# Ordering steps behind three engines' queues, placing the ternary weights, and the lead of the gathered rows in a 12-sublayer decoder

## The chip, the cores and the metric

The kernel runs on one core of one Trainium2 chip. The metric is the time of one execution on the device in microseconds (us), as the median of several executions. A core has a matrix engine (TensorE, PE; its weight loads are listed as PEld), a vector engine (VectorE, DVE), a scalar engine (ScalarE, ACT), a general engine (GpSimd, POOL) and a sync engine (SyncE, SP) that here issues DMAs. Each engine works through its own queue in order; engines wait for each other by semaphores.

## The reference

A decoder of four layers with three sublayers each, on 8192 tokens of width D = 128. Each sublayer is added to its input and normalised. The change touches the first three sublayers, and the planning ahead of the last one:

```python
# L0 attn: mixture of experts, the best 2 of 8 for each token
logits = x @ gate_w + gate_b;  probs = softmax(logits)
topw, topi = top_k(probs, 2);  topw = topw / topw.sum(-1)
hid = gelu(einsum('nd,edf->enf', x, w1) + b1)
out = einsum('enf,efd->end', hid, w2) + b2
x = layernorm(x + sum over the two experts of out * topw)
# L0 xattn: one head, context of 64 rows per sequence
x = layernorm(x + softmax(q @ k.T * scale) @ v)
# L0 ffn: ternary weights
t(w) = w + (clip(round(w / mean(abs(w))), -1, 1) - w)
x = layernorm(x + gelu(x @ t(W1).T + b1) @ t(W2).T + b2)
...
# L3 ffn: the best 1 of 8 experts, with a capacity for each expert
```

## The kernel before

The tokens lie in 16 chunks of 512 (four tiles of 128 tokens). The twelve sublayers run in the order of a list at the end of `tile_decoder`. The tile framework orders each engine's instructions by a scheduler; `tc.issue_after(ins)` puts what is made in its block behind `ins` on that instruction's own engine, without making it wait for anything else. Without such an edge, the scheduler may place an instruction among others as it likes, so far as data allow.

**Mixture of experts** (class `Sorted`, L472). Only the chosen experts are computed. A `plan` sorts the pairs of token and expert into groups of 256 rows that share an expert. There are two batches: chunks 0 to 4 with 27 groups and chunks 5 to 15 with 51. For each group n, `all_groups` (L860) does these steps:
- `load(n + 2)` (L727): SP reads a register with the expert's number and issues two DMAs, weights `rw` (512 KB, L738) and biases `aux` (66 KB, L739).
- `rows(n + 3)` (L742): DVE copies the row indices (`rat`, L755), POOL issues two indirect DMAs that gather 128 rows each (L757) into one of eight places in the four `aux` tiles.
- `turn(n + 1)` (L763): PE transposes the rows (`ebT_ps`, L768), DVE copies them (`ebT`, L770).
- `hidden(n)` (L772): PE multiplies (`h_ps`, L782), ACT applies GELU (L784).
- `output(n - 1)` (L787): PE multiplies (`yg`, L795), DVE adds the bias (`yo`, L796), SP stores 128 KB to `l_rout` in DRAM (L797).
- `between`: a hook; here `context` (L920) loads the context `cin` (256 KB per chunk) in the last 32 groups.
- The steps laid aside: the plan of the next batch, whose last step is due four groups before the end (`total - 4`), and the sums (`finish`, L802) of the batch before, spread by `stretch`. They are queued behind the last instruction of `Sorted` on each engine.

`finish` reads back, tile by tile, the two outputs of each token: DVE copies indices (`fat`, L815), POOL gathers two `got` tiles (L817), DVE adds them to x (`r`, L827 and L829) and takes statistics (L830). At the end of a chunk `end` (L832 to L847) finds 1/sqrt by integer steps on DVE (`fln`, `rt_u`, L348 to L357) and applies the normalisation in `ln_apply` (L372): on ACT (L378, after one more DVE operation `lns`, L375), on POOL or on DVE (L380).

What remains of the sums after the groups is `moe_end`. `moe_done(c)` (L936) runs it until chunk c is finished.

**One-head cross attention with the ternary FFN** (`xattn_single`, L984). It makes the ternary weights of the FFN first: `ternary(n)` (L1062 to L1080) for two matrices of 128 x 512, each with one ACT operation, a reduction (`terns`, L1067), a matmul (L1069) and eight DVE operations. Its loop (L1108 to L1116) interleaves the steps of several chunks: scores(i+1), summed, turned(i-2), turned_weights(i), projections(i+2), summed, hidden(i-2), summed, values(i), sources(i+3), output(i-2), summed. `summed` takes one step of `moe_end`, so the MoE's sums end in this loop, four steps (one chunk) in a turn. `sources` calls `moe_done`. The matmuls `y` at L1048 end the attention of a chunk; r at L1054 adds them to x. PE's operations that the prediction names are the score values `v_ps` (L1003, L1008), the transposes `xT_ps` (L325) and the FFN's `h_ps` (L1093) and `y` (L1103).

**Masked attention and switch.** The plan of the last sublayer's first batch (`switch_begin`) is made during the masked attention (`mha`, L1130): the hook `aside` calls `kept` (L1916), which takes a few steps at each of four places of a chunk, behind instructions that `mha` hands to it (`seen`). Its operations are named `plan`, `pln`, `pli`, `plw`.

Of the kernel before, what the change touches and what calls it, by code (L numbers as in the profile page):

```python
# [22 lines left out]
P = 128  # L23
# [208 lines left out]


@with_exitstack
def tile_decoder(ctx: ExitStack, tc: tile.TileContext, a, out):
# [9 lines left out]
    mm = nc.tensor.matmul  # L245
    V, A, G = nc.vector, nc.scalar, nc.gpsimd

# [38 lines left out]
    def load_weights(n):  # L286

        if 0 < n < 11:
            name = LAYER_WEIGHTS[n - 1]
            parts = []  # L290
            for o in range(0, _NBLOCKS[name], 8):
                k = min(8, _NBLOCKS[name] - o)
                parts.append(work("wts", (P, k, P), f"w_{name}{o}"))
                nc.sync.dma_start(out=parts[-1], in_=a["w_" + name][:, o : o + k, :])
            W[n] = parts[0] if len(parts) == 1 else parts

    def table(name, shape, src):
# [14 lines left out]
    make_identity(nc, ident)  # L312


    def bank(name):
# [156 lines left out]
    class Sorted:  # L472
# [4 lines left out]
        def __init__(s, which, top, batches, src, wg, bias, act, cap=None, store=False, scattered=None):  # L477
            s.which, s.top, s.batches, s.src, s.wg, s.bias, s.act, s.cap, s.store = which, top, batches, src, wg, bias, act, cap, store
            s.at, s.loaded, s.done, s.carry = {}, {}, set(), None
# [322 lines left out]
        def finish(s, b):  # L802
# [29 lines left out]
            def end(i):  # L832
                r, st = sums.pop(i)
                got.pop(i)
                f = sm.tile([P, 4, TPC], F32, tag="fln", name="fln")
                mv = f[:, :2].rearrange("p a t -> p (a t)").rearrange("p (t a) -> p t a", a=2)
                v, y = f[:, 2], f[:, 3]
                for t in range(TPC):
                    V.bn_aggr(mv[:, t, :], st[:, t, :])  # L839
                s.dve = V.tensor_scalar(v, mv[:, :, 1], LN_EPS, None, ALU.add)  # L840
                yield
                for ins in rsqrt_steps(v, TPC, y):
                    s.dve = ins
                    yield
                ln_apply(cs[i], r, mv, y, s.store, on_act=True)
                s.done.add(cs[i])
                yield  # L847
# [12 lines left out]
        def all_groups(s):  # L860
# [3 lines left out]
            s.ring = work("e", (P, 8, 2, D), "yo")  # L864
            for n in range(3):
                s.rows(n)
# [4 lines left out]
            for b in range(nb):  # L871
# [68 lines left out]

# [41 lines left out]


    def xattn_single():  # L984
        w = W[1]
        scale = 1.0 / math.sqrt(D)

        st = {}
        bv = bias_rows(row("l0xbv"), 0, "bv1")
        ring = work("e", (P, 4, TPC, D), "v1")  # L990
# [66 lines left out]

        b2 = bias_rows(row("l0fb2"), 1, "b2t")
        tern = W[2]
        wt = work("tab", (P, 2, FK, P), "tern")  # L1060

        def ternary(n):  # L1062
            src = tern[:, 4 * n : 4 * n + 4, :].rearrange("p k m -> p (k m)")
            t = work("tmp", (P, 512), "absw")
            s = sm.tile([P, 1], F32, tag="terns", name="terns")
            A.activation(t, src, AF.Abs)
            V.tensor_reduce(s, t, AX.X, ALU.add)  # L1067
            ps = bank("tern_ps")
            mm(ps[:, 0:1], sq[:, 2, :], s, start=True, stop=True)  # L1069

            V.tensor_scalar(s, ps[:, 0:1], 1.0 / (D * FF), 1e-8, ALU.mult, ALU.max)
            V.reciprocal(s, s)
            df = wt[:, n].rearrange("p k m -> p (k m)")
            V.tensor_scalar(df, src, s, None, ALU.mult)
            V.tensor_scalar(df, df, -1.0, 1.0, ALU.max, ALU.min)

            V.tensor_scalar(df, df, 12582912.0, None, ALU.add)
            V.tensor_scalar(df, df, 12582912.0, None, ALU.subtract)
            V.tensor_tensor(df, df, src, ALU.subtract)
            V.tensor_tensor(df, df, src, ALU.add)  # L1080

        def summed(_):
            next(moe_end, None)

# [23 lines left out]
        for i in range(-3, NC + 2):  # L1108
            for step, c in (
# [19 lines left out]

    def mha(prepare, wv, finish, mask=None, diff=False, aside=lambda c, k, seen: None):  # L1130

# [164 lines left out]
        nlam = lam_neg() if diff else None  # L1296
        on, late, spread = range(NC), (), None
        for c in range(-2, NC + 1):
            last = finish(c - 1, st[c - 1]) if c - 1 in on else iter(())
            behind = None  # L1300
            if c in on:
                behind = weights(c, 0)
            for _ in late:
# [3 lines left out]
            if c - 1 in on:  # L1307
                values(c - 1, 1)
            aside(c, 0, (behind, spread))
# [5 lines left out]
            aside(c, 1, (seen, spread))  # L1315
            if c in on:
                weights(c, 1)
                behind = values(c, 0)
            aside(c, 2, (behind, spread))
            if c + 1 in on:  # L1320
                scores(c + 1, 1)
                split_maxima(c + 1)
            if c + 2 in on:
                spread = project(c + 2)
            next(last, None)
# [5 lines left out]
            late = last if diff else ()  # L1331
            aside(c, 3, (seen, spread))
            st.pop(c - 1, None)
# [581 lines left out]

    def kept(c, k, seen):  # L1916

# [46 lines left out]
```

## Time and profile before

| | |
|---|---|
| median of 18 runs | 3300.52 us (3290.14 to 3305.32) |
| profiled execution | 3298.73 us |
| its span, from the first to the last instruction | 3297.0 us |
| mean granted PE clock | 0.948 |
| busy, PE / PEld / DVE / ACT / POOL | 2909.4 / 2119.3 / 2016.3 / 1642.1 / 1463.5 us |
| first group's `h_ps` / last group's, about | 65 / 434 us |
| cross attention and ternary FFN, about | 438 to 735 us |
| masked attention, about | 2700 to 3035 us |

The page gives for each group of instructions the line, engine, operation, tile written and tiles read. "Idle before" is the time that the engine stood still ahead of an instruction, and the arrow names what ended it. A list of waits sums these. In a table of windows each engine's busy time in a stretch stands beside the granted clock (1.00 is full speed), the share of the DMA engines that was busy and what they moved. Tile names are shown without their numbers.

### The profile page before, as it was taken

Reading aid. Unit: us, or ns where it says so; the run is one execution under the profiler, and the core shown is the slowest. Engines: PE = TensorE matmul, PEld = TensorE weight load, DVE = VectorE, ACT = ScalarE, POOL = GpSimd, SP = SyncE. Lnnn points to the kernel's source line nnn. Section 1 sums busy time; section 2 is a strip of 40 time slices with the busy share of each in tenths; the row PEclk is TensorE's granted clock in tenths of the full one; section 3 lists DMA queues with packets and bytes.
Section 4 is the critical chain, followed back from the end, with each engine's and each line's share of the span. In section 5 each row is a group of like instructions: output and inputs, shape, how many; then the busy total and the mean of one; then the engine's idle time right before and its main releaser. Section 6 shows DMA issues by size and latency. Waiting matters only on the chain. (4 is left out here: it accounts for less than half of the span.)

```text
span 3297.0 us, 110598 instructions
## 1 busy us (share of the span) xinstructions
PE 2909.4 (88%) x47136; PEld 2119.3 (64%) x47136; DVE 2016.3 (61%) x7344; ACT 1642.1 (50%) x3138; POOL 1463.5 (44%) x1500
## 2 busy tenths in 40 slices
PE   5898888998899899999999989998999569998983
PEld 3788755666666677766677767774444336766883
DVE  3732256766777666532346655666888886675245
ACT  3443355765444455433345645553445555654443
POOL 2565554334555444311134453557566323436234
PEclk9999988999999899999999999999999789998997
DMA  4577731000000200000000000000000000002674
GB/s 132 157 201 209 223 83 30 21 8 3 3 3 10 84 4 4 6 1 1 1 15 4 4 5 4 4 6 7 1 1 2 8 1 16 18 14 71 193 236 135
DMA packets 142461, 159.26 MB, mean 48 GB/s; under 512 B 16720, under 2 KB 118096, under 8 KB 141968
## 3 DMA queue, kind: packets, MB, share of 16 engines
q1 hardware_dynamic: 128064, 123.66, 12.7%
q0 software_dynamic: 13184, 27.03, 3.0%
q8 instruction: 370, 6.06, 0.8%
q10 hardware_dynamic: 720, 1.50, 0.1%
q14 instruction: 123, 1.01, 0.1%
HBM read 121.45 MB, written 30.67 MB: 46 GB/s over the span
## 5 line engine op out<-in xcount | busy, mean ns | idle before, releaser
L1213 DVE TENSOR_REDUCE m<-s_ps 128x8 f32<-128x512 f32 x640 | 397.5, 683 | 143.6 <-PE s_ps L1441 49.3
L1262 ACT ACTIVATE e<-t_ps 128x512 f32<-128x512 f32 x640 | 330.0, 602 | 150.3 <-PE t_ps L1255 149.8
L1280 PE MATMUL av_ps<-vx,e 128*64 128x18 f32 (+1 forms) x10240 | 335.8, 215 | 6.2 <-issue 6.0
L1280 PEld LDWEIGHTS av_ps<-vx,e 128*64 128x64 f32 x10240 | 317.8, 139 | 26.1 <-issue 19.0
L784 ACT ACTIVATE hT<-h_ps,aux 128x256 f32<-128x256 f32 x496 | 206.4, 469 | 247.2 <-issue 157.9
L1157 POOL TENSOR_SCALAR eb<-qT,small 128x512 f32<-128x512 f32 x80 | 130.6, 1632 | 422.4 <-ACT qT L960 200.6
L817 POOL DMA_INDIRECT got<-l_rout,fat x192 | 192.5, 1003 | 222.4 <-DVE fln L839 64.4
L1243 PE MATMUL t_ps<-eb,kT 32*64 32x128 f32 x10240 | 281.9, 285 | 4.6 <-DVE m L1213 2.3
L380 POOL TENSOR_SCALAR x<-xb,lnmv,ln_y 128x128 f32<-128x128 f32 x240 | 188.4, 797 | 175.6 <-DVE ln_y L345 169.1
L782 PE MATMUL h_ps<-ebT,rw 128*128 128x256 f32 x992 | 246.9, 394 | 19.5 <-DVE ebT L770 16.1
L795 PEld LDWEIGHTS yg<-rw,hT 128*128 128x128 f32 x1984 | 244.9, 194 | 6.9
L1243 PEld LDWEIGHTS t_ps<-eb,kT 32*64 32x64 f32 x10240 | 199.3, 132 | 71.5 <-DVE m L1213 25.5
L795 PE MATMUL yg<-rw,hT 128*128 128x128 f32 x1984 | 244.7, 277 | 0.0
L1205 PE MATMUL s_ps<-eb,qT 32*64 32x256 f32 x5120 | 216.9, 397 | 20.2 <-POOL eb L1157 9.6
L757 POOL DMA_INDIRECT aux<-in_x_dram,rat x156 | 159.0, 1019 | 125.6 <-DVE rat L755 43.2
L782 PEld LDWEIGHTS h_ps<-ebT,rw 128*128 128x128 f32 x992 | 185.3, 197 | 45.2 <-DVE ebT L770 20.1
L380 POOL TENSOR_SCALAR x<-r,lnmv,ln_y 128x128 f32<-128x128 f32 x100 | 79.6, 808 | 296.9 <-DVE ln_y L345 250.5
L796 DVE TENSOR_TENSOR yo<-yg,aux 128x256 f32<-128x256 f32 x124 | 52.4, 422 | 254.6 <-PE yg L795 254.5
L1285 DVE RECIPROCAL rc<-av_ps 128x32 f32<-128x32 f32 (+1 forms) x192 | 61.7, 321 | 236.9 <-PE av_ps L1280 236.5
L1155 ACT ACTIVATE eb<-qT,small 128x512 f32<-128x512 f32 x160 | 106.8, 715 | 128.4 <-POOL qT L1382 123.7
L1157 POOL TENSOR_SCALAR eb<-kT,small 128x512 f32<-128x512 f32 x80 | 144.8, 1810 | 21.5 <-ACT kT L962 11.0
L1205 PEld LDWEIGHTS s_ps<-eb,qT 32*64 32x64 f32 x5120 | 113.5, 134 | 60.2 <-issue 15.6
(443 smaller groups left out, 6502.1 us busy)
## 6 DMA issues: line engine op xcount, KB each, us to landing
rw<-in_l0w_dram SPq DMA_DIRECT2D x78, 512.0 KB
rw<-in_l3w_dram SPq DMA_DIRECT2D x46, 512.0 KB
l_rout<-yo SPq DMA_DIRECT2D x124, 128.0 KB
aux<-xd SPq DMA_DIRECT2D x46, 128.0 KB
aux<-in_l0b_dram SPq DMA_DIRECT2D x78, 66.0 KB
xd<-vx SPq DMA_DIRECT2D x5, 1024.0 KB
x<-in_x_dram SPq DMA_DIRECT2D x16, 256.0 KB
cin<-in_ctx_dram SPq DMA_DIRECT2D x16, 256.0 KB
```

What stands on the lines that cost most here:

```text
L380: (V if on_dve else G).tensor_scalar(X[c][:, t, :], r[:, t, :], mv[:, t, 0:1], y[:, t : t + 1], ALU.subtract, ALU.mult)
L757: s.gather = G.indirect_dma_start(out=eb[:, i, :], out_offset=None, in_=x[:, :], in_offset=bass.IndirectOffsetOnAxis(ap=at[:, i : i + 1], ...
L782: s.pe = mm(ps[:, j * GR : (j + 1) * GR], w1[:, (k + j) * P : (k + j + 1) * P], ebT, start=True, stop=True)
L784: s.act_ins = A.activation(hT[k + j], ps[:, j * GR : (j + 1) * GR], s.act, bias=v[:, k + j : k + j + 1])
L795: s.pe = mm(y[:, i * P : (i + 1) * P], hT[k][:, i * P : (i + 1) * P], w2[:, k, :], start=(k == 0), stop=(k == FK - 1))
L817: s.gather = G.indirect_dma_start(out=got[i][k][:, t, :], out_offset=None, in_=s.rout[b][:, :], in_offset=bass.IndirectOffsetOnAxis(ap=at[ ...
L1157: ins = (G if h == 2 else V).tensor_scalar(dst, x, mine, None, ALU.mult)
L1205: mm(ps[g][j * S : (j + 1) * S, u * 256 : (u + 1) * 256].rearrange("p (h k) -> p h k", h=4), rows32(s["q"], g)[:, b], rows32(s["eb"], g)[: ...
L1213: last = V.tensor_reduce(s["m"][:, g, 2 * hf : 2 * hf + 2, :].rearrange("p t h -> p (t h)"), ps[g].rearrange("p (n k) -> p n k", k=S), AX. ...
L1243: mm(ps[g][i * S : (i + 1) * S].rearrange("p (a u j q) -> p a u j q", u=2, a=2, j=2)[:, :, u, j, :], rows32(s["k"], g)[:, b], rows32(s["eb ...
L1262: last = A.activation(e[:, g, :], ps[g], AF.Exp, scale=scale)
L1280: mm(av[j * S : (j + 1) * S, 8 * (u - u0) + n, :], ev[:, n // 2, n % 2, u, j, :], vx[:, 2 * (2 * hf + u) + j, n, :], start=True, stop=True,)
```

## The change

1. `V`, `A` and `G` become wrappers (`Recorded`) that remember the last instruction issued on VectorE, ScalarE and GpSimd. A new `behind(V, A, G)` queues a block behind those.
2. Each step of `moe_end` (in `moe_done` and in `summed`) and each step of `switch_begin` (in `kept`) is put behind all three. `kept` no longer gets instructions from `mha`.
3. The MoE reads the rows of a group five groups ahead instead of three (the switch, whose rows are sorted already, stays at three); the plan of the next batch is due two groups earlier.
4. The ternary weights' source (l0f, 512 KB) is loaded when 30 groups are left. The weights and two bias rows are made in 12 steps, one at each odd number of groups left below 24, behind V, A, G and the MoE's last matmul. In `xattn_single` they are no longer made.
5. After `all_groups` the rest of the sums normalises on POOL instead of ACT (`slack`).

```diff
+class Recorded:
+    def __init__(self, engine):
+        self.engine, self.last = engine, None
+    def __getattr__(self, name):
+        method = getattr(self.engine, name)
+        def call(*args, **kwargs):
+            ins = method(*args, **kwargs)
+            self.last = getattr(ins, "ins", None) or self.last
+            return ins
+        return call
...
-    V, A, G = nc.vector, nc.scalar, nc.gpsimd
+    V, A, G = Recorded(nc.vector), Recorded(nc.scalar), Recorded(nc.gpsimd)
...
-        if 0 < n < 11:
+        if 0 < n < 11 and n not in W:
...
+    def behind(*engines):
+        stack = ExitStack()
+        for e in engines:
+            if e.last:
+                stack.enter_context(tc.issue_after(e.last))
+        return stack
...
-                ln_apply(cs[i], r, mv, y, s.store, on_act=True)
+                ln_apply(cs[i], r, mv, y, s.store, on_act=not s.slack)
...
-            for n in range(3):
+            far = 3 if s.sorted else 5
+            for n in range(far):
                 s.rows(n)
...
-                    aside.append([s.plan(b + 1), s.plan_costs(b + 1), 0, 0, total - 4])
+                    aside.append([s.plan(b + 1), s.plan_costs(b + 1), 0, 0, total - far - 1])
...
-                    if n + 3 < N:
-                        s.rows(n + 3)
+                    if n + far < N:
+                        s.rows(n + far)
...
-    moe.between = context
-
     def moe_top2():
...
         moe.all_groups()
+        assert next(making, None) is None
+        moe.slack = True
 
     def moe_done(c):
         while c not in moe.done:
-            next(moe_end)
+            with behind(V, A, G):
+                next(moe_end)
...
+    def ternary(n):
+        src = W[2][:, 4 * n : 4 * n + 4, :].rearrange("p k m -> p (k m)")
...
+        A.activation(t, src, AF.Abs)
+        yield V.tensor_reduce(s, t, AX.X, ALU.add)
+        ps = bank("tern_ps")
+        moe.pe = mm(ps[:, 0:1], sq[:, 2, :], s, start=True, stop=True)
+        yield
+        V.tensor_scalar(s, ps[:, 0:1], 1.0 / (D * FF), 1e-8, ALU.mult, ALU.max)
+        V.reciprocal(s, s)
+        df = FIRST["wt"][:, n].rearrange("p k m -> p (k m)")
+        V.tensor_scalar(df, src, s, None, ALU.mult)
+        yield V.tensor_scalar(df, df, -1.0, 1.0, ALU.max, ALU.min)
+        V.tensor_scalar(df, df, 12582912.0, None, ALU.add)
+        yield V.tensor_scalar(df, df, 12582912.0, None, ALU.subtract)
+        V.tensor_tensor(df, df, src, ALU.subtract)
+        yield V.tensor_tensor(df, df, src, ALU.add)
+
+    def made_first():
+        FIRST["wt"] = work("tab", (P, 2, FK, P), "tern")
+        for n in range(2):
+            yield from ternary(n)
+        FIRST["bv"] = bias_rows(row("l0xbv"), 0, "bv1")
+        yield
+        FIRST["b2"] = bias_rows(row("l0fb2"), 1, "b2t")
+        yield
...
+    def before_single(left):
+        context(left)
+        if left == 30:
+            with moe.after(moe.sp):
+                moe.sp = load_weights(2)
+        if left < 24 and left % 2:
+            with behind(V, A, G), moe.after(moe.pe):
+                moe.dve = next(making, None) or moe.dve
+
+    moe.between = before_single
...
         def summed(_):
-            next(moe_end, None)
+            with behind(V, A, G):
+                next(moe_end, None)
...
-            if i in (-3, -2):
-                ternary(i + 3)
...
-    def kept(c, k, seen):
+    def kept(c, k):
...
-        with ExitStack() as behind:
-            for i in seen:
-                if i:
-                    behind.enter_context(tc.issue_after(i))
-            for _ in range(steps):
+        for _ in range(steps):
+            with behind(V, A, G):
                 next(switch_begin, None)
```

More of the change, by code (lines that the diff above doesn't have):

```diff
@@ L293, in load_weights @@
                 parts.append(work("wts", (P, k, P), f"w_{name}{o}"))
-                nc.sync.dma_start(out=parts[-1], in_=a["w_" + name][:, o : o + k, :])
+                ins = nc.sync.dma_start(out=parts[-1], in_=a["w_" + name][:, o : o + k, :])
             W[n] = parts[0] if len(parts) == 1 else parts
+            return ins
     def table(name, shape, src):
@@ L478, in __init__ @@
             s.which, s.top, s.batches, s.src, s.wg, s.bias, s.act, s.cap, s.store = which, top, batches, src, wg, bias, act, cap, store
-            s.at, s.loaded, s.done, s.carry = {}, {}, set(), None
+            s.at, s.loaded, s.done, s.carry, s.slack = {}, {}, set(), None, False
             s.row_tiles, s.turned, s.between, s.stretch, s.rest = {}, {}, None, 1, None
@@ L981, in bias_rows @@
         return both[:32, 0, :], both[:32, 1, None, :].to_broadcast([32, 4, D])
+    FIRST = {}
+    def ternary(n):
+        src = W[2][:, 4 * n : 4 * n + 4, :].rearrange("p k m -> p (k m)")
+        t = work("tmp", (P, 512), "absw")
+        s = sm.tile([P, 1], F32, tag="terns", name="terns")
+        A.activation(t, src, AF.Abs)
[20 more added lines that the diff above has]
+        yield
+    making = made_first()
+    def before_single(left):
[7 more added lines that the diff above has]
+    moe.between = before_single
     def xattn_single():
@@ L988, in xattn_single @@
         st = {}
-        bv = bias_rows(row("l0xbv"), 0, "bv1")
         ring = work("e", (P, 4, TPC, D), "v1")
@@ L1055, in values @@
             layernorm(c, r, on_act=True)
[L1058 to L1080, printed above, removed]
+        wt, bv, b2 = FIRST["wt"], FIRST["bv"], FIRST["b2"]
         def summed(_):
-            next(moe_end, None)
+            with behind(V, A, G):
+                next(moe_end, None)
         def turned(c):
@@ L1128, in rows32, with mha @@
         return t[32 * g : 32 * g + 32]
-    def mha(prepare, wv, finish, mask=None, diff=False, aside=lambda c, k, seen: None):
+    def mha(prepare, wv, finish, mask=None, diff=False, aside=lambda c, k: None):
         dh = 16 if diff else 8
@@ L1296, in mha @@
         nlam = lam_neg() if diff else None
-        on, late, spread = range(NC), (), None
+        on, late = range(NC), ()
         for c in range(-2, NC + 1):
             last = finish(c - 1, st[c - 1]) if c - 1 in on else iter(())
-            behind = None
             if c in on:
-                behind = weights(c, 0)
+                weights(c, 0)
             for _ in late:
@@ L1308, in mha @@
                 values(c - 1, 1)
-            aside(c, 0, (behind, spread))
+            aside(c, 0)
             seen = scores(c + 1, 0) if c + 1 in on else None
@@ L1314, in mha @@
                 project_v(c + 1)
-            aside(c, 1, (seen, spread))
+            aside(c, 1)
             if c in on:
                 weights(c, 1)
-                behind = values(c, 0)
-            aside(c, 2, (behind, spread))
+                values(c, 0)
+            aside(c, 2)
             if c + 1 in on:
@@ L1323, in mha @@
             if c + 2 in on:
-                spread = project(c + 2)
+                project(c + 2)
             next(last, None)
@@ L1331, in mha @@
             late = last if diff else ()
-            aside(c, 3, (seen, spread))
+            aside(c, 3)
             st.pop(c - 1, None)
```

## The prediction

> **What bounds the kernel now.** I read the clock and span first (3297.0 us, mean clock 0.948; the execution itself took 3298.73 us, 1.8 under the median of 3300.52), then the slices, then tables by stage. The edits touch three stages: the MoE groups (64 to 438 us), the one-head cross attention and ternary FFN (438 to 735) and the end of the masked attention (2920 to 2960). On TensorE (PE) the instructions are the same in both kernels, and so is their order behind the first 2,390 of 38,758.
>
> *Groups.* PE's timeline of an undisturbed stretch gives the floor of one group:
>
> ```profile
> 224.70 1.90 PE L782 MATMUL h_ps<-ebT,rw 128*128 128x256 f32 x8
> ...
> 228.44 1.89 PE L782 MATMUL h_ps<-ebT,rw 128*128 128x256 f32 x8
> ...
> 232.17 1.89 PE L782 MATMUL h_ps<-ebT,rw 128*128 128x256 f32 x8
> ...
> 237.72 1.90 PE L782 MATMUL h_ps<-ebT,rw 128*128 128x256 f32 x8
> ```
>
> 228.44 - 224.70 = 3.74 and 232.17 - 228.44 = 3.73 us, and then a group of 5.55. From h of group 22 (188.76) to h of group 77 (433.8) the mean is 245.0 / 55 = 4.45: 55 x (4.45 - 3.73) = 40 us above the floor. The waits of 200 to 440 us (total, times, longest) say who takes them:
>
> ```profile
> POOL got L817 <- DVE r L827: 38.6, 11, 13.5
> PEld ebT_ps L768 <- DMA aux<-in_x_dram,rat: 30.2, 22, 3.2
> ...
> PE ebT_ps L768 <- DMA aux<-in_x_dram,rat: 25.3, 18, 3.0
> ```
>
> PE waits 25.3 us for gathered rows. The rows come late because POOL's queue holds a `got` gather that waits for a free buffer (up to 13.5 us), and the row gathers stand behind it. One of these on PE's timeline:
>
> ```profile
> 297.63 1.95 PE L795 MATMUL yg<-rw,hT 128*128 128x128 f32 x16
> 302.60 0.48 PE L768 MATMUL ebT_ps<-ident,aux 128*128 128x128 f32 x1 [3.02 <-DMA aux<-in_x_dram,rat]
> ```
>
> and the windows (busy PE, PEld, DVE, ACT, POOL, then clock, DMA share, GB/s) around it, with a well-fed one ahead of them from another answer:
>
> ```profile
> 220.00:240.00 20.00, 18.33 (x125) 16.88 (x124) 4.40 (x16) 7.82 (x19) 13.96 (x14) 1.00 0.82 242
> ```
>
> ```profile
> 300.00:305.00 5.00, 2.14 (x6) 1.58 (x7) 0.56 (x3) 0.00 (x0) 3.92 (x4) 0.71 0.90 277
> 305.00:310.00 5.00, 5.00 (x25) 4.55 (x24) 0.07 (x1) 1.68 (x4) 0.00 (x0) 0.60 0.18 57
> ```
>
> The gap of 3.02 us is followed by a clock of 0.60 to 0.71. The 20-us windows' clocks of .83, .91, .91 and .83 in 200 to 440 cost about 20 x (.17+.09+.09+.17) = 10 us. 25.3 + 10 = 35 of the 40.
>
> *Cross attention.* Here chunk follows chunk by the start of the first `y` matmul (L1048): 27.0 us from chunk 2 to 3, a mean of (624.2 - 508.86)/6 = 19.2 for the next six, and 14.5 to 14.9 once the MoE sums are done, with PE 100% busy. Among the sums PE, ACT and POOL wait for late DVE work: on PE's timeline, then POOL's, then in the waits of 440 to 640:
>
> ```profile
> 443.57 0.58 PE L1003 MATMUL v_ps<-vx 32*128 32x512 bf16 x1 [4.48 <-DVE terns L1071]
> ```
>
> ```profile
> 497.64 1.01 POOL L817 DMA_INDIRECT got<-l_rout,fat  x1 [0.30 <-issue]
> 505.87 1.00 POOL L817 DMA_INDIRECT got<-l_rout,fat  x1 [7.22 <-DVE fln L839]
> ```
>
> ```profile
> POOL got L817 <- DVE fln L839: 63.5, 8, 10.2
> ACT x L378 <- DVE lns L375: 46.3, 10, 8.3
> ```
>
> **The parts.**
>
> 1. *Rows five groups ahead.* The same gathers are issued two groups (7.5 us at the floor) earlier. Their buffers allow it: the eight halves of `aux` give group n+5 the place of group n-3, whose transposes are four groups back. The lead in front of the transpose grows from two groups to four, 15 us, over the longest hold of 13.5. So PE's 35 us would go, and the floor would give -40. What is late next is the DMA. A group moves 512 + 66 (weights, biases) + 128 (rows) + 128 (store) KB, about 50 of `got`, and in the last 32 groups 128 of context: 1.01 MB, which in 3.73 us is 271 GB/s. The trace held 242 in the window above and up to 265 in the other MoE stage; at 255 these groups take 3.97 us, 32 x 0.24 = +7.6. The l0f and l1a weights now move among the groups too: 0.9 MB at 250 GB/s, +3.6. Sum -40 + 11 = **-28**. Bounds: -40 (no drag) and -8 (the 25.3 us turn into waits for weights and only most of the clock loss goes).
>
>    The Trainium skill (TensorE: Matmul & The Clock Gate, "HAM oscillation — how this bites in real kernels") puts the harmful gap at over about 3.4 us. By it gaps of 3.0 cost no clock, and this term would be -18; the 0.60 after 3.02 us says otherwise, and the trace decides.
>
> 2. *Plan of batch 1 due in 21 groups instead of 23.* DVE is 15.9 to 19.4 of 20 us busy at 120 to 180, so the plan's work sets the pace there (5.0 us a group), and packing it tighter leaves two faster groups behind it: 21 x 5.12 + 2 x 3.73 = 23 x 5.0. **0**, with +5 if it now delays transposes' copies.
>
> 3. *Ternary weights among the groups.* 16 DVE operations, per matrix .13+.15+.46+.42+.42+.42+.68+.69 = 3.4 us, two 6.7 us, leave 443 to 456, where DVE is 15.0 of 20 us busy and PE lost 4.48. They go where DVE is 4 to 6 of 20 busy, hidden by PE's 17.7 of 20. If that cover fails, each of the 12 steps holds `ebT` copies by at most one operation pair, 1.4 us: +8. **-5** (the 4.48 and a little clock); bounds -9, +3.
>
> 4. *Steps queued behind V, A and G; normalising the rest on POOL.* `moe_done` and `summed` may no longer be hoisted or spread by the scheduler, so DVE does xattn's own work in the order written, and 14 chunks' LN applies (56) leave ACT for POOL. Their prices:
>
> ```profile
> L378 ACT ACTIVATE x<-r,lns,fln x128: 477/481/536, 356.5 to 3292.8; 128x128 f32<-128x128 f32 x128
> ```
>
> ```profile
> L380 POOL TENSOR_SCALAR x<-r,lnmv,ln_y x100: 782/792/1541, 652.0 to 1681.8; 128x128 f32<-128x128 f32 x100
> ```
>
>    Four cost 1.9 us on ACT and 3.2 on POOL, and the `lns` operation on DVE goes. ACT no longer stands up to 8.3 us with its own softmax and GELU queued behind an apply; instead `got` gathers (1.00 + 0.30 each, 2.6 a pair) are queued behind the applies on POOL, and the transposes of `x` behind both. POOL's need per chunk is 4 x 2.6 + 3.2 = 13.6, under 19.2.
>    - The slump of 27.0 us should shrink to about 21, like its neighbours: **-6**; bounds -9, and +10 if the three chunks' applies (3 x 3.1) in front of the gathers of batch 1 are paid in full.
>    - The steady chunks: by the compiled order I count x ready about 8.5 us behind `y` (fln 2.6, first apply 0.8, a pair 2.6, three applies 2.4), and some 10 us of PE work behind that: 17.8 to 18.7, plus 0 to 2 for a slow clock after PE's wait. Against 19.2 over seven chunks: **-3**; bounds -8, +10.
>
>    The Trainium skill (GPSIMD Engine Reference, "Engine selection") calls one-input elementwise work on POOL roughly line-rate against VectorE. By it four applies would be near DVE's 1.1 us and the steady term about -10; the 792 ns row decides.
>
> 5. *The switch's plan in the masked attention.* The last LN chain, now in front of the plan's operations, took 5.4 us (2955.0 to 2960.4) interleaved with them and 4.0 (2930.4 to 2934.4) alone; `av_ps` starts there are 13.1 and 14.3 us apart against about 9.5 later: **-3**; bounds -8, +4.
>
> Sum: -28 + 0 - 5 - 6 - 3 - 3 = **-45**: 3298.7 - 45 = 3254 for a profiled execution, and **3255** for the median.
>
> **Rivals.**
> - *DMA and POOL become the bound of the groups.* For: 271 GB/s would be needed at the end, POOL needs 2.6 for the rows and 0.7 for sums (14 pairs of `got` over 51 groups) of 3.73 us. Against: the other MoE stage runs at 3.73 with 246 GB/s. The groups give only -12, the rest -8: 3280.
> - *All of it*: groups at the floor (-40), xattn chunks at 17 us (7 x -2.2 = -15), the slump and the ternary in full (-9, -9): 3227.
> - *Slower: POOL's queue holds `x` in the cross attention.* Each chunk's x waits for the dearer applies (3.2 - 1.9 = 1.3) and one gather pair (2.6) more: 3.9 us over the 11 chunks of batch 1 = +43. Against the groups' -28 and the ternary's -5 that is +10: 3310. It decides from 3 us a chunk, (28 + 5)/11. Against it: the applies start as soon as their statistics do, and ACT's 46.3 us of waiting went through the same chain.
> - *The lead is not real* (gathers still behind held `got` gathers, which moved ahead with them): groups 0, the rest -8 to 0: 3296, no change.
>
> **How the numbers follow.** Forecast 0.48 (3236 to 3270), all of it 0.18, DMA and POOL 0.18, no lead 0.06, slower 0.10. This kernel's measurement can tell about 0.2%, 6.6 us. The no-lead case is half faster: faster 0.48 + 0.18 + 0.18 + 0.02 = 0.86, same 0.04, slower 0.10. The range leaves out most of "slower" and the tail of "all of it": 3218 to 3292.
>
> **What would show it.** Right: h starts 3.8 to 4.0 us apart at 200 to 430, the wait of `ebT_ps` for gathered rows under 8 us, clock near 1.00 there; 434 - 30 for the last h; no PE wait on `terns`; chunk intervals of the cross attention at 17 to 19 and none over 22. Wrong: PE waiting for `rw`, DMA share over 0.9 with groups still at 4.4; PE waiting more than 3 us a chunk at `xT_ps` for POOL's `x`; chunk intervals over 20.

## The result, and the profile after

The changed kernel takes 3341.02 us (median of 7), the kernel before 3300.87 (43): ratio 1.0122, 95% interval [1.0108, 1.0136]. It is slower by 1.2%, where 1.4% faster was forecast and the range ended at 3292. The spans of the two profiled executions differ by 3338.0 - 3297.0 = 41.0 us. Four marks on PE's timelines say where it comes from (us from the span's start):

| mark | before | after | difference of the stage |
|---|---|---|---|
| last block of `yg` of the groups | 434.2 | 404.7 | -29.5 |
| last attention `y` of the cross attention | 706.3 | 725.7 | +49.0 (272.0 became 321.0) |
| first `s_ps<-mf,half` (the mask) of the masked attention | 2720.4 | 2741.7 | +1.9 |
| first `h_ps` of the switch | 3042.2 | 3082.6 | +19.1 (321.8 became 340.9) |
| end of the span | 3297.0 | 3338.0 | +0.6 |

*Groups.* All operations of DVE, ACT and POOL now carry the line L243, that of the wrapper, so they are read by tile. On PE's timeline the groups stand 3.73 us apart (215.89 - 212.16):

```profile
212.16 1.89 PE L806 MATMUL h_ps<-ebT,rw 128*128 128x256 f32 x8
...
215.89 1.89 PE L806 MATMUL h_ps<-ebT,rw 128*128 128x256 f32 x8
```

Two executions of the kernel before, in the table above and in e6 below, differ by 10 us in the first mark (434.2 and 424.0), so the groups' -29.5 is known no better than that.

No wait of PE for gathered rows is left among the waits of 200 to 440 us; the largest wait of PE for a DMA there is the one for weights:

```profile
PE h_ps L806 <- DMA rw<-in_l0w_dram: 5.3, 2, 4.1
```

and the DMA carries more than in any 20-us window of 200 to 440 us before (at most 244 GB/s). A window of 40 us; the next one has 270 GB/s:

```profile
280.00:320.00 40.00, 38.51 (x266) 35.98 (x265) 12.81 (x54) 17.41 (x42) 27.15 (x28) 1.00 0.90 278
```

*Cross attention.* Aligned by the first `y` matmul of each chunk's attention, the stage lost its time in two places, and the rest of it changed by -3 us in all:

| chunks | before | after | difference |
|---|---|---|---|
| 3 to 9 | 508.86 to 624.20, 19.2 us each | 478.91 to 616.22, 22.9 each | +22 us |
| 9 to 13 | 624.20 to 682.99, 14.7 us each | 616.22 to 704.98, 22.2 each | +30 us |

The same four stretches as windows (the clock is the third column from the end), the kernel before first:

```profile
508.90:624.20 115.30, 102.79 (x650) 69.16 (x649) 79.75 (x519) 73.87 (x148) 46.86 (x48) 0.88 0.10 28
624.20:683.00 58.80, 58.80 (x435) 39.16 (x434) 45.28 (x274) 48.68 (x97) 15.88 (x19) 1.00 0.06 19
```

```profile
478.90:616.20 137.30, 110.42 (x650) 74.46 (x649) 88.50 (x517) 66.76 (x127) 68.50 (x73) 0.80 0.09 24
616.20:705.00 88.80, 75.47 (x434) 50.33 (x433) 52.53 (x299) 45.90 (x86) 39.68 (x45) 0.81 0.07 20
```

The clock was already 0.88 before in the first stretch; after, it is 0.80. In the second stretch PE was never idle before: POOL's last `got` gather started at 631.53, and PE waited for none of the sums' last tiles. After, that gather starts at 664.62, and PE still waits for POOL's `x` at 688.15.

Among the waits of 408 to 740 us are these:

```profile
ACT xT L243 <- PE xT_ps L349: 126.5, 24, 8.8
POOL got L243 <- DVE r L243: 77.5, 15, 10.0
DVE r L243 <- PE y L1150: 72.0, 13, 8.4
...
PE xT_ps L349 <- POOL x L243: 45.7, 45, 3.7
```

PE's waits for POOL's `x` are new, and DVE waits for the FFN's `y` longer than before (72.0 us instead of 14.8 in 440 to 740); POOL's gathers waited for DVE before too (63.5 us for `fln` in 440 to 640). ACT's wait for the transposes follows from PE's. Read as a loop: PE waits for POOL's `x`; POOL's gathers, which stand ahead of `x` in its queue, wait for DVE's adds (`r`), which free their buffers; DVE waits for PE's `y` of the FFN (L1150), because that addition is queued ahead of the sums' adds. DVE's timeline, the addition of `y` at the start of a turn, a sum's add, and the next addition of `y`:

```profile
540.10 0.69 DVE L243 TENSOR_TENSOR r<-y,x 128x512 f32<-128x512 f32 x1 [4.35 <-PE y L1150]
...
546.34 0.34 DVE L243 SCALAR_TENSOR_TENSOR r<-got,plw,x 128x128 f32<-128x128 f32 x1
...
562.96 0.69 DVE L243 TENSOR_TENSOR r<-y,x 128x512 f32<-128x512 f32 x1 [7.92 <-PE y L1150]
```

PE's timeline of the same turn:

```profile
552.51 0.48 PE L349 MATMUL xT_ps<-ident,x 128*128 128x128 f32 x1 [3.43 <-POOL x L243]
...
553.45 1.65 PE L1150 MATMUL y<-tern,vx 128*128 128x128 f32 x6
555.92 0.48 PE L349 MATMUL xT_ps<-ident,x 128*128 128x128 f32 x1 [0.82 <-POOL x L243]
...
557.73 5.19 PE L1150 MATMUL y<-tern,vx 128*128 128x128 f32 x26
```

and POOL's timeline what the tiles stand behind: four gathers, the first of which waits for the sum's add, and a pair of gathers between the first apply and the other three.

```profile
546.70 0.99 POOL L243 DMA_INDIRECT got<-l_rout,fat  x1 [8.65 <-DVE r L243]
...
551.65 0.80 POOL L243 TENSOR_SCALAR x<-r,fln 128x128 f32<-128x128 f32 x1
552.63 1.08 POOL L243 DMA_INDIRECT got<-l_rout,fat  x1 [0.17 <-DVE lnst L243]
554.02 1.00 POOL L243 DMA_INDIRECT got<-l_rout,fat  x1 [0.30 <-issue]
555.07 2.35 POOL L243 TENSOR_SCALAR x<-r,fln 128x128 f32<-128x128 f32 x3
```

The windows of 5 us in this turn show the other part of the loss, the clock (third column from the end; 0.99 in the window ahead of these, 547 to 552 us):

```profile
552.00:557.00 5.00, 3.38 (x10) 2.00 (x10) 2.76 (x17) 0.00 (x0) 4.48 (x6) 0.50 0.13 39
557.00:562.00 5.00, 4.70 (x22) 4.54 (x22) 0.00 (x0) 0.59 (x1) 2.50 (x3) 0.50 0.08 26
562.00:567.00 5.00, 5.00 (x40) 3.27 (x39) 3.80 (x26) 2.86 (x7) 0.00 (x0) 0.98 0.01 3
```

PE is idle for 3.43 us, and then works for 10 us at half speed.

*End of the masked attention.* PE's first instruction of the switch, of before and then of after:

```profile
3038.45 0.66 PE L768 MATMUL ebT_ps<-ident,aux 128*128 128x128 f32 x2 [2.78 <-DMA aux<-xd]
```

```profile
3078.99 0.66 PE L792 MATMUL ebT_ps<-ident,aux 128*128 128x128 f32 x2 [15.76 <-DMA aux<-xd]
```

Its rows were scattered by POOL, 40 scatters at 0.97 + 0.30 us. Before, they ran from 2971.18 to 3033.78 and none but the first waited over 0.31 us; after, from 2996.57 to 3074.04 with holes. Counted from the stage's start (2720.4 and 2741.7) the first scatter is 4 us later, and the scatters take 15 us longer. Lines of POOL's timeline after:

```profile
3047.09 0.97 POOL L243 DMA_INDIRECT xd<-x,pli  x1 [6.02 <-DVE rc L243]
...
3062.56 0.97 POOL L243 DMA_INDIRECT xd<-x,pli  x1 [3.02 <-DVE pli L243]
```

### The profile page after: what moved, and what is told of

Read it like the earlier page. It is cut to its first block, busy times and chain, and to the rows that moved or that the text cites. A ratio compares the mean times of both kernels' runs of the same rounds, so it can differ in the third digit from the quotient of the medians.

```text
span 3338.0 us, 110655 instructions
## 1 busy us (share of the span) xinstructions
PE 2931.5 (88%) x47136; PEld 2134.3 (64%) x47136; DVE 2039.3 (61%) x7330; ACT 1621.2 (49%) x3082; POOL 1507.6 (45%) x1556
## 5 line engine op out<-in xcount | busy, mean ns | idle before, releaser
L243 DVE TENSOR_REDUCE m<-s_ps 128x8 f32<-128x512 f32 (+1 forms) x656 | 404.1, 677 | 154.1 <-PE s_ps L1485 49.3
L243 ACT ACTIVATE e<-t_ps 128x512 f32<-128x512 f32 x640 | 330.0, 601 | 150.5 <-PE t_ps L1300 150.0
L243 POOL TENSOR_SCALAR eb<-qT,small 128x512 f32<-128x512 f32 x80 | 130.4, 1630 | 423.0 <-ACT qT L243 344.8
L243 ACT ACTIVATE hT<-h_ps,aux 128x256 f32<-128x256 f32 x496 | 207.1, 470 | 225.6 <-issue 110.2
L243 POOL DMA_INDIRECT got<-l_rout,fat x192 | 194.9, 1015 | 218.9 <-DVE r L243 121.2
L243 POOL TENSOR_SCALAR x<-xb,lnmv,ln_y 128x128 f32<-128x128 f32 x240 | 188.0, 795 | 177.1 <-DVE ln_y L243 173.5
L806 PE MATMUL h_ps<-ebT,rw 128*128 128x256 f32 x992 | 246.0, 392 | 23.7 <-DVE ebT L243 13.2
L243 POOL DMA_INDIRECT aux<-in_x_dram,rat x156 | 159.8, 1024 | 114.1 <-PE h_ps L806 49.3
L243 POOL TENSOR_SCALAR x<-r,lnmv,ln_y 128x128 f32<-128x128 f32 x100 | 79.6, 809 | 286.5 <-DVE ln_y L243 259.6
L243 DVE RECIPROCAL rc<-av_ps 128x32 f32<-128x32 f32 (+1 forms) x192 | 61.7, 321 | 238.9 <-PE av_ps L1325 238.7
L243 DVE TENSOR_TENSOR yo<-yg,aux 128x256 f32<-128x256 f32 x124 | 52.4, 422 | 253.8 <-PE yg L819 253.8
L243 ACT COPY xT<-xT_ps 128x512 f32<-128x512 f32 x128 | 76.9, 601 | 240.3 <-PE xT_ps L349 239.9
L243 ACT ACTIVATE eb<-qT,small 128x512 f32<-128x512 f32 x160 | 106.8, 715 | 128.3 <-POOL qT L243 123.3
L243 POOL TENSOR_SCALAR eb<-kT,small 128x512 f32<-128x512 f32 x80 | 144.7, 1809 | 21.7 <-ACT kT L243 19.6
```

The costliest lines, as they stand in the source:

```text
L243: ins = method(*args, **kwargs)
L806: s.pe = mm(ps[:, j * GR : (j + 1) * GR], w1[:, (k + j) * P : (k + j + 1) * P], ebT, start=True, stop=True)
```

## The experiments

Two theories stood at first for the cross attention: P, that the applies on POOL are the cause, and S, that the order behind DVE's queue is. A third, C, came later: that the slow clock after each of PE's waits is a large part of it. For the planning there was K: the three edges make it late.

The runs came in five sets, each with the kernel before measured beside it; the ratios are to that. In two of the sets (e1 to e4, e13 to e16) that kernel itself took 3382 and 3385 us instead of about 3300, with more idle time of PE under "issue" (18.0 us ahead of `av_ps` in e4, 7.6 in e10, which are the same kernel) and slower groups whatever the kernel (from the 24th of the 78 groups to the last 234 to 236 us in e4, e14 and e15, 210 to 213 in the changed kernel, e5, e9 and e10). The study did not find why. So stages are compared within a set only; those two sets have no trace of the kernel before. "Stage" is from the last block of `yg` to the last attention `y` (the expectations count it from the end of that block, 3.5 us less); "planning" is from the first `s_ps<-mf,half` of the masked attention to the first `h_ps` of the switch.

| run | ratio, 95% interval | before, us | stage | planning |
|---|---|---|---|---|
| e1 kept of before | 1.0066 [1.0042, 1.0091] | 3382 | 329.4 | 364.2 |
| e2 applies on ACT | 0.9972 [0.9956, 0.9988] | 3382 | 301.5 | 372.5 |
| e3 sums free | 0.9948 [0.9927, 0.9970] | 3382 | 288.2 | 375.0 |
| e4 rows five alone | 0.9996 [0.9977, 1.0015] | 3382 | 301.3 | 363.0 |
| e5 after again | 1.0132 [1.0108, 1.0157] | 3297 | 323.2 | 344.0 |
| e6 before again | one run, 3284.11 us | 3297 | 268.2 | 321.5 |
| e7 sums free and ACT | 1.0008 [0.9995, 1.0020] | 3297 | 277.9 | 344.2 |
| e8 applies on DVE | 0.9876 [0.9857, 0.9895] | 3297 | 243.3 | 343.8 |
| e9 DVE, kept of before | 0.9810 [0.9784, 0.9837] | 3299 | 243.7 | 322.5 |
| e10 rows five again | 0.9930 [0.9910, 0.9950] | 3299 | 269.7 | 322.3 |
| e11 applies in one piece | 1.0117 [1.0079, 1.0155] | 3299 | 313.5 | 345.8 |
| e12 DVE, sums free | 0.9950 [0.9924, 0.9976] | 3299 | 268.3 | 341.4 |
| e13 short fill | 1.0052 [1.0034, 1.0070] | 3385 | 330.5 | 370.3 |
| e14 ternary in single | 0.9987 [0.9970, 1.0004] | 3385 | 301.6 | 362.9 |
| e15 kept free | 0.9987 [0.9974, 1.0000] | 3385 | 291.4 | 376.3 |
| e16 sums behind G | 0.9918 [0.9898, 0.9938] | 3385 | 281.9 | 370.2 |
| e17 one piece, filled | 1.0029 [1.0014, 1.0044] | 3301 | 286.3 | 344.2 |
| e18 one piece again | 1.0110 [1.0076, 1.0143] | 3301 | 314.4 | 340.8 |

**e1.** The changed kernel, with `kept` and `mha` as in the kernel before.

> The changed kernel with only the switch's planning during the masked attention put back (kept and mha as before). Theory K: a plan step queued behind the last instruction of all three engines comes later, the scatters of the switch's rows on POOL end later, and the first group of the switch waits 15.8 us for its rows instead of 2.8. Then the time is about 20 us below the changed kernel: 3321, and from the first s_ps of the masked attention to the first h_ps of the switch it takes about 322 us instead of 341. Rival: the plan is late because of something before it; then 3341 and still about 341.

Planning took 364.2 us beside 372.5 and 375.0 of e2 and e3 in the same set: K holds, at 8 to 11 us in this set.

**e2, e3.** Each undoes one half of the cross attention's change.

```diff
-                ln_apply(cs[i], r, mv, y, s.store, on_act=not s.slack)
+                ln_apply(cs[i], r, mv, y, s.store, on_act=True)
```

```diff
-            with behind(V, A, G):
-                next(moe_end, None)
+            next(moe_end, None)
```

> The changed kernel with the remaining sums normalised on ACT again; steps still queued behind all three engines. From the last yg of the groups to the last attention y of the cross attention it took 268.5 us before and 317.5 in the changed kernel. Theory P: POOL's applies, dearer and behind the gathers, are the cause; then this stage falls back to about 270 and the time to about 3293. Theory S: the order is the cause, a loop in which the sums' adds on DVE stand behind the addition of the FFN's y, the y behind transposes of x on PE, the x behind the gathers on POOL and the gathers behind the adds; then only the 1.3 us that an apply of a chunk is cheaper come back, some 11 to 15 us: about 3328.

> The changed kernel with the steps of the sums (moe_done, summed) no longer queued behind V, A and G; the applies stay on POOL. Theory S: the loop is gone, the stage from the last yg to the last y falls from 317.5 to about 270 and the time to about 3296. Theory P: the POOL applies stay the limit; stage over 305, time over 3328.

Both theories were half right: against e1's stage of 329.4, ACT gives back 28 us and the free order 41. e4, whose cross attention is that of the kernel before, has 301.3 in this set, so either cut takes the whole loss away: it needs both together.

**e4, e10.** The kernel before with `far = 5` (and `total - far - 1`), run in two sets.

> The kernel before with the rows read five groups ahead (and the plan due two groups earlier) and nothing else. The prediction's term: the groups end 28 us earlier and nothing is given back: 3273. Rival: of the sums that run beside the groups nothing is done earlier, so the cross attention has the same sums left and keeps its 268.5 us, but the gathers of sums are held longer beside faster groups: groups -28, stage +10: 3283.

> The kernel before with the rows five groups ahead alone, once more, on a chip in which the kernel before takes about 3300 us. The prediction's term: PE's wait for gathered rows gone, the last yg about 25 us earlier, ratio 0.992. As in its first run: PE's wait gone but waits for weights and ACT in its place, ratio 1.000.

In e10 the ratio is 0.993, some 23 us, with a stage of 269.7: the prediction's first term, nothing given back. In e4 the last `yg` came at 435.4 instead of 408.4, PE's wait for rows was gone too, but it waited 9.5 us for `rw` and 7.7 for its own issue ahead of `h_ps` and `yg` (64 to 435 us), and nothing was gained. In that set the groups were held by something else, which the study did not find.

**e5, e6.** The two kernels themselves again.

> The changed kernel itself, so that its ratio and its stages stand beside those of the other runs of the same chip. Ratio to before 1.012 as at first; from the last yg of the groups to the last attention y about 49 us longer than in the kernel before.

> The kernel before, for its stages on this chip. Ratio 1.000; PE waits some 25 us for gathered rows in 200 to 440 us.

1.0132 and a stage 55 us longer repeat the result.

**e7.** e2 and e3 together.

> The changed kernel with both undone in the cross attention: sums not queued behind the engines, and applies on ACT. Undoing either alone brought the ratio from 1.012 to 0.997 (ACT) and 0.995 (order). If they are two costs that add, both together give 0.995 + 0.997 - 1.012 = 0.980. If they are one loop that needs both, and each cut opens it, both together give about what one gave: 0.993 to 0.998.

1.0008: no sum of two costs, but not what one gave either. The stage is 277.9, by 10 us over e6's 268.2, although the ternary weights have left it; where these 10 us come from stays open.

**e8, e12.** Applies on DVE, with the order and without.

```diff
-                ln_apply(cs[i], r, mv, y, s.store, on_act=not s.slack)
+                ln_apply(cs[i], r, mv, y, s.store, on_act=not s.slack, on_dve=s.slack)
```

> The changed kernel with the remaining sums normalised on DVE (1.1 us a chunk instead of 3.2 on POOL), steps still queued behind all three engines. If the place behind the gathers in POOL's queue is what closes the loop, this opens it as ACT did: ratio 0.997. If the length of the chain is what counts whatever the engine, DVE's queue, which waits for the FFN's y, closes it too: 1.005 to 1.012.

> Applies on DVE, new planning, but the steps of the sums not queued behind the three engines. If the order is worth something of its own once POOL is out of the chain, this is slower than with the order (0.9876): by the run with both undone (1.0008) up to 1.000. If the gain came from DVE's applies alone, 0.988.

The stage falls to 243.3, 25 us under e6's. Without the order it is 268.3, against 243.7 of e9, which has the order in the same set. So with DVE's applies the order is worth some 25 us; with POOL's the stage is some 50 us longer than before's. Where the sums are free (e3, e7, e12) the last chunks follow at 14.1 to 14.9 us again; in the changed kernel they follow at 20.2 to 24.0. With the order and DVE's applies (e8) all ten chunks from 3 to 13 take 14.7 to 17.5 us each, sums and all. PE waits less for `x` there: in one turn of e8 1.21 us (at 513.51), and the 26 `y` matmuls behind it take 3.98 us instead of 5.19.

**e9.** e8 with `kept` and `mha` of before.

> The two costs found so far both taken out: remaining sums normalised on DVE (0.9876 with the new planning) and the switch's planning during the masked attention as before. If the planning costs the same 20 to 23 us here (from the first s_ps of the masked attention to the first h_ps of the switch 321 us instead of 344), the ratio is 0.9876 - 0.0065 = 0.981. If the loss in the masked attention came from what ran before it, 0.987.

0.981, 3238.52 us against 3298.73 in its set: the fastest of all, 60 us under the kernel before, with the planning at 322.5, where e11 and e12 in the same set have 345.8 and 341.4.

**e11, e18.** The gathers moved out from between the applies, nothing else.

```diff
             for n in range(nt + LATE + 3):
+                for x in ends:
+                    next(x, None)
                 if n < nt:
-                    read(n)
+                    with behind(G) if s.slack else nullcontext():
+                        read(n)
...
                         ends.append(end((n - LATE) // TPC))
-                for x in ends:
-                    next(x, None)
+                        next(ends[-1])
                 yield
```

> The changed kernel with one pair of gathers moved: on POOL, the four applies of a chunk now stand in one piece, where the changed kernel puts a pair of got gathers (2.6 us) between the first and the other three. Everything else as changed. Theory: x is on the chain that sets the pace, so 11 chunks x 2.6 = 29 us and the clock after PE's wait come back, ratio 1.013 - 0.009 - 0.002 = 1.002. Rival: the chain's other members (3.2 us of applies, the gathers behind held buffers) set the pace, and the pair is hidden: 1.010 to 1.013.

> The kernel with the applies in one piece, as e11, beside the filled one on the same chip: 1.012 as at first.

1.0117 and 1.011: the theory missed, the pair is not what sets the pace. PE's wait for `x` did not shrink (430 to 740 us: 50.6 us in e18, 42.2 in the changed kernel), and the clock stayed low (0.80 and 0.83 in e18's windows of 500 to 560 and 560 to 620 us).

**e13, e17.** Useless transposes of the identity where PE waits, 18 in the changed kernel, then 38 on top of e11 (they are extra work, and no result of them is used).

```diff
+            ps = bank("xT_ps")
+            if c > 2:
+                for _ in range(38):
+                    nc.tensor.transpose(ps[:, :P], ident, ident)
```

> The changed kernel with 18 transposes of the identity (about 4.0 us, no result is used) on PE ahead of each chunk's first transpose of x, where PE waits for POOL. Theory C: of the 49 us that the stage lost, some 21 are the slow clock that follows each wait of 3.4 to 3.7 us; with PE busy in the wait the clock in 500 to 680 us goes from 0.80 to over 0.93 and the ratio from 1.013 to about 1.007, though PE does more. Rival: the chain through DVE, the gathers and POOL sets the pace and PE's slower y is covered by it; then the clock rises and the ratio stays at 1.011 or over.

> The kernel with the applies in one piece (e11), and 38 transposes of the identity (0.11 us each by the run before, 4.3 us, no result is used) on PE ahead of each chunk's first transpose of x. The first fill was too short: 2.1 us, and the wait moved to the second tile, behind the gathers. Theory C: with PE busy in the wait the clock in 500 to 680 us is over 0.93 instead of 0.80, the y matmuls of the FFN run at full speed, and the ratio is 0.006 below the run beside it. Rival: the pace is set by the chain through DVE, the gathers and POOL; the clock rises, the ratio stays within 0.002 of the run beside it.

e13 tells nothing: the fill took 2.1 us and the wait (3.12 us) moved to the second tile. e17 tells: 1.0029 against 1.011 beside it. PE, the clock and one turn:

```profile
500.00:560.00 60.00, 59.06 (x468) 44.16 (x467) 47.96 (x279) 34.25 (x64) 37.64 (x41) 1.00 0.11 29
560.00:620.00 60.00, 59.30 (x484) 44.80 (x484) 45.34 (x262) 35.32 (x67) 36.88 (x40) 1.00 0.12 31
```

```profile
553.95 4.31 PE L1068 MATMUL xT_ps<-ident 128*128 128x128 f32 x38
558.09 0.49 PE L1070 MATMUL xT_ps<-ident,x 128*128 128x128 f32 x3
558.82 0.33 PE L1070 MATMUL xT_ps<-ident,x 128*128 128x128 f32 x1 [0.23 <-POOL x L243]
559.08 0.39 PE L1157 MATMUL y<-vx 32*128 32x512 bf16 x1
559.39 3.84 PE L1160 MATMUL y<-tern,vx 128*128 128x128 f32 x32
```

32 matmuls in 3.84 us, 0.12 each, against 26 in 5.19, 0.20 each. The chunks follow at 18.7 us instead of 21.4 to 24.1, though PE does 4.3 us more in each. With the clock held up the stage is 28 us shorter (314.4 to 286.3): chunks 3 to 9 take 114.0 us instead of e18's 134.0, chunks 9 to 13 75.6 instead of 86.0. The first is before's 115.3; the second is still 17 us over before's 58.8, because the sums are still there. The 28 us are not all new with the change, since the clock of the kernel before was low in part of this stage too (0.88).

**e14.** e9 with the ternary weights and bias rows made in the cross attention.

```diff
-        if left < 24 and left % 2:
-            with behind(V, A, G), moe.after(moe.pe):
-                moe.dve = next(making, None) or moe.dve
...
+        for _ in making:
+            pass
         wt, bv, b2 = FIRST["wt"], FIRST["bv"], FIRST["b2"]
```

> The fastest kernel so far (applies on DVE, planning of before: 0.981) with the ternary weights and the two bias rows made at the start of the cross attention again instead of among the groups. The prediction's term was 5 us, bounds -3 and 9: 0.9825. Rival: the place costs nothing, since DVE is not what the first chunks wait for: 0.981.

**e15.** e8 with the planning's steps behind nothing (`next(switch_begin, None)` alone).

> Applies on DVE, and the new planning steps of the switch queued behind nothing at all. With the three edges 0.9876, with the planning of before (each step behind one instruction of the attention) 0.981. Theory: the three edges put each step behind whatever was issued last on DVE, and the scatters, which close the planning, late; without any edge the scheduler places them as early as data allow and the first group of the switch waits as little as before: 0.981, or slower if free steps then break into the attention's own DVE work: 0.985.

Both ratios are 0.9987, outside what either expectation allowed: in this set the gain of e8 and e9 is not there (e15's stage is 291.4, e8's 243.3), so that gain is shown only for the sets in which the kernel before takes about 3300 us. The two differ in planning too, which comes later; up to there they are e9 with and without the new place. The stage is 301.6 against 291.4: by one trace of each the new place is worth 10 us, the term being 5. In planning, e15 is 13 us slower than e14, and 6 slower than e13 and e16 with the three edges. The scatters end early (PE's first `h_ps` of the switch 5.7 us behind the attention's end, 6.8 in e14), but the attention takes 370.7 us instead of 356.1. So having edges is not the fault; before's, each behind one instruction chosen in `mha`, were better than three and than none. In this set the scatters wait for `pli` with before's edges too (39.2 us in e14, 38.7 in e13, between 2900 and 3150 us), so such holes by themselves do not tell the orders apart here.

**e16.** `behind(G)` instead of `behind(V, A, G)` in `moe_done` and `summed`, applies on POOL.

> The changed kernel with the sums' steps queued behind POOL's last instruction alone; applies still on POOL. The instruction order with the edge on DVE alone is that of the changed kernel but for one gather. Theory: the edge on DVE is the one that closes the loop, so without it this is like the run without edges (1.7% under the changed kernel): 0.995. If POOL's own order closes it: 1.012.

0.9918, stage 281.9: without the edges on DVE and ACT the sums run ahead, and PE's wait for `x` in 430 to 740 us is 4.1 us, where e1 had 42.6. The run takes the edges on DVE and ACT away together. That DVE's is the one that closes the loop fits the waits above and the instruction order that the expectation names, but no run took it away alone.

## Why the prediction was wrong, point by point

- **Rows five ahead: right, in three sets of four.** -28 forecast; with all edits the last `yg` comes 29.5 us earlier in the two first traces and 21.6 between e6 and e5, and the rows alone bring about 23 us (e10); in e4's set they brought nothing. The clock is 1.00 there, and the DMA carried 270 to 278 GB/s, more than the 255 of the estimate. The 40 us above the floor were miscounted by a little: from 188.76 to the last group's `h_ps` at 432.51 there are 54 groups of 4.51, 42 us.
- **Ternary weights: right in sign, perhaps too small.** 5 forecast, 10 measured by one trace of each (e14 against e15).
- **Steps in order, applies on POOL: wrong, and the main error.** -9 forecast, and with the ternary weights' -5 a stage 14 us shorter; it became 49 us longer. The step that failed is the steady chunks: "17.8 to 18.7, plus 0 to 2 for a slow clock after PE's wait", "Against 19.2 over seven chunks". It failed twice.
  - *The pace and its clock.* Chunks 3 to 9 took 22.9 us each instead of 19.2: +22 us. The chain was counted well enough: with the clock held up the chunks follow at 18.7 us (e17). The clock term was mis-sized, 0 to 2 us a chunk for about 4. PE waits for `x` in every chunk (one wait of 3.4 to 3.7 us or several shorter ones), and some 10 us at half speed follow in the turns shown. The groups' rows had shown just this (0.60 after a gap of 3.02 us), and the prediction priced it there, at 10 us, and hardly here. Even by its own numbers the term was too good: 17.8 to 20.7 has its middle at 19.2, which is 0 over seven chunks and not -3.
  - *The number of chunks.* The prediction had seen that chunks follow at 14.5 to 14.9 us once the sums are done, and by pricing seven chunks alone took it that they would be done as early as before. With each step held in its written place the sums last to chunk 13, and chunks 9 to 13 go at their pace, 22.2 us instead of 14.7: +30 us, the larger part of the loss, for which the sum had no term.
  - The slump of chunk 2 to 3 went from 27.0 to 23.7 us, -3 instead of -6.
- **"POOL's need per chunk is 13.6, under 19.2"** compared busy times. POOL was not short of time (busy for 68.5 of the 137.3 us of chunks 3 to 9); it was the loop through DVE, where the sums' adds stand behind an addition that waits for PE, that kept `x` late. Each of four cuts (e2, e3, e8, e16) took the loss away; moving one pair of gathers (e11) did not.
- **Switch's planning: wrong.** -3 forecast from DVE's normalisation chain, +19 measured, 19 to 23 taken back by e9 (against e12 and e11). The step priced DVE alone. What ends last there is POOL's queue of 40 scatters, 40 x 1.28 = 51 us, which can't start before DVE's `pli` and which stops wherever `pli` is late: counted from the stage's start it began 4 us later, and it took 77.5 us instead of 62.6. Which of the three edges does it stays open; that fewer edges are not better is shown by e15.
- **The rivals.** The slower one, "POOL's queue holds x in the cross attention", with 3.9 us a chunk and +10 in all, named the place, and was given 0.10. That its 3.9 x 11 = 43 us come near the 49 measured is luck: the pair of gathers in it is not what sets the pace (e11), it had no clock in it, and of its eleven chunks six lost 3.7 us each and four 7.5. The lost 19 us of the planning were in no rival.

## What to carry to other kernels

An idle gap of PE that returned in every turn of a loop cost twice here: the gap (3.43 us), and the slow stretch behind it (10 us at 0.50); price both from the clock of such a gap elsewhere in the same trace. When a step is queued behind the last instruction of an engine, ask what that instruction waits for, and follow it around: if the way leads back to the step, its pace is the whole loop, whatever the busy shares say. Ask also how long such side work will last: a stage in which it ends early has two paces, and holding the work in order can stretch the slow one over all of it (22.2 us a chunk instead of 14.7). And where an edit makes a producer of indices later, cost the longest queue that hangs on them, here POOL's scatters, not the producer.

## What the runs showed of the hardware that was not expected

- Work that computes nothing made the kernel faster: 38 transposes in PE's wait raised the clock from 0.80 and 0.83 to 1.00 (windows of 60 us) and took 0.8% off (1.011 to 1.0029).
- The Trainium skill (TensorE: Matmul & The Clock Gate, "HAM oscillation — how this bites in real kernels") describes such a loop, in which every turn's wait throttles the next turn's matmuls, with gaps over about 3.4 us. The waits of 3.43 us here agree with it, the gap of 3.02 us in the kernel before (0.60 behind it) lies under that limit. Nor must it be one gap: in another turn of the changed kernel the longest wait was 1.68 us, with shorter ones behind it, PE was busy for 2.76 of 5 us, and the next 5 us had a clock of 0.50.

The windows of that turn in the changed kernel:

```profile
572.00:577.00 5.00, 2.76 (x27) 1.95 (x28) 4.19 (x30) 2.72 (x5) 4.08 (x4) 0.88 0.15 41
577.00:582.00 5.00, 3.80 (x16) 2.80 (x15) 2.47 (x11) 0.94 (x2) 4.48 (x6) 0.50 0.09 26
```
